# A different hand-written step list for the two later passes of a fused Fourier-layer kernel

## Chip, core and metric

The kernel runs on one core of one Trainium2 chip. The metric is the device time of one execution in microseconds; the kernel before was timed three times. One more execution of it was recorded by the hardware profiler, and all rows below come from that one.

## What is computed

64 images of 256 x 256 pixels go through a tokenizer (four Fourier layers with 32 channels), are joined with 77 text tokens of width 256, and pass through one attention layer and one feed-forward layer that only the better-scored half of the tokens enter. Cut to what matters here:

```python
for i in range(4):                                   # v: [64, 32, 256, 256]
    x_ft = rfft2(v)
    out_ft[:, :, :12, :12]  = einsum('bixy,ioxy->boxy', x_ft[:, :, :12, :12], W1)
    out_ft[:, :, -12:, :12] = einsum('bixy,ioxy->boxy', x_ft[:, :, -12:, :12], W2)
    x1 = irfft2(out_ft)
    x2 = einsum('bcxy,cd->bdxy', v, w_w[i]) + w_b[i]
    v  = x1 + x2
    v  = (v - mean(v)) * rsqrt(var(v) + 1e-5) * bn_g[i] + bn_b[i]    # over all 64 images
    if i < 3: v = relu(v)
h = einsum('bcxy,cu->bxyu', v, q_w) + q_b            # then text, attention, feed-forward
```

Everything is float32.

## The kernel before

An image with its 32 channels is 8.4 MB, so the 64 images stay in DRAM (`vd`, two copies used in turn) and stream through the core once for each of three passes, `layer(0)`, `layer(1)` and `layer(2)`. Between passes, `mix` (line 409) multiplies the kept frequencies with the layer's weights and derives the normalisation. Pass 0 makes its input from the raw pixels and only stores. Passes 1 and 2, the later passes, load every image and store every image. After them comes the tail (line 930 on): attention and feed-forward, which loads the last result once.

**One image in a later pass.** It is cut into eight tiles t = 0 to 7 of [128 partitions, 2048 numbers], 1 MB each. `run` (line 784) gives each step a short name:

- `ld` t (line 631) loads a tile into a buffer of pool `li` (four buffers, name `vin`) as two DMAs of 512 KB on SyncE's queue (SP).
- `sp` h, `spT` h (lines 637, 646) expand the mixed frequencies (`ams`) along x and transpose them on VectorE into `y_`; half h serves four tiles.
- `pre` t (line 655) adds the inverse transform along y (L661, 16 matmul instructions) and the channel product of the loaded tile (L672, 32 instructions) in PSUM.
- `evA` t, `evB` t (line 679) rectify one half each from PSUM into `vo`, a buffer of pool `lo`. The suffix says where: `.a` is ScalarE (L684), `.d` is VectorE (L686). These are the rectified chunks.
- `st` t (line 690) stores the tile to DRAM as two DMAs of 512 KB, also on SP (L693).
- `turn` t (line 695) transposes it on VectorE into half of `t32`, a buffer of pool `lt` that holds two tiles. These are the transposed pairs.
- `prod` t, `sqA`, `sqB` (lines 703, 715) multiply the tile with the next layer's weights (L709) and sum the squares on ScalarE (L720).
- `y` k, k = 0 to 7 (line 724), sum the forward transform along y over all eight tiles (L731), and `half`, `zt0`, `zt1`, `x`, `xo`, `xs` (lines 738 to 782) finish and store the kept frequencies. `am` (line 622) loads and scales the mixed frequencies of a later image.

**Order.** No scheduler orders a pass: `tc.manual_schedule()` (line 838) keeps the program's order on every engine. That order is the text `ORDER[1]` (line 135), which is walked once per image index b (line 802). A mark `@1` runs a step for image b+1, `@-1` for image b-1. Each of TensorE (PE), VectorE (DVE), ScalarE (ACT) and SP has its own queue and takes its own steps in the list's order; an instruction whose data or buffer is not ready holds up all that follow on its engine.

**What makes a step wait.** PSUM is a ring of four two-bank slots (`take`, line 580); `pre`, `prod` and `y` take two, `sp` and `x` one, and the steps that read a slot empty give it back. A load waits until the `pre` that used the same `vin` buffer four loads earlier has read it. An eviction waits until the earlier tile in its `vo` buffer has been stored (landed in DRAM), turned and multiplied. A store waits for its two evictions. In addition, SP's DMAs use eight completion semaphores in turn, and each DMA waits for the one eight places earlier, so that at most eight are under way. In the compiled order of the kernel before this stands as a wait on `DMAHW0` to `DMAHW7` at each DMA.

The pools that matter are opened at line 540: `("lo", 4)` for `vo` and `("lt", 6)` for `t32`, in all three passes.

Of the kernel before, what the change touches and what calls it, by code (L numbers as in the profile page):

```python
# [34 lines left out]
def _tables():  # L35
# [97 lines left out]
    "evB7.a evA7.a prod5 sqB5 prod6 sqA6 st4 x@-1 sqB6 turn6 sqA5 pre1@1 st7 xo@-1 pre0@1 "  # L133
    "evA1.a@1 evB1.d@1 evB0.a@1 xs@-2 evA0.d@1 prod7 sqB7 turn7 sqA7 prod1@1 sp1@1 sqA1@1 "
), (
    "pre5 sqB7@-1 zt1@-1 sqA7@-1 pre6 evA5.a ld2@1 st4 evB5.d st5 turn4 evA6.a prod5 x@-1 "
    "evB6.a sqB5 prod6 sqA5 xo@-1 turn5 pre2@1 sqA6 turn6 sqB6 prod4 evA2.a@1 evB2.d@1 "
    "sqB4 ld0@1 ld7 sqA4 pre0@1 evB0.d@1 ld3@1 prod2@1 st6 evA0.a@1 turn2@1 sqB2@1 sqA2@1 "
    "pre3@1 ld1@1 evA3.a@1 st2@1 evB3.d@1 pre7 evB7.d prod3@1 ld5@1 evA7.a sqA3@1 turn7 "
    "pre1@1 st0@1 am@2 sqB3@1 prod0@1 evA1.a@1 evB1.d@1 sqA0@1 st7 sp1@1 st1@1 ld4@1 y0 "  # L140
    "spT1@1 y1 ld6@1 turn0@1 turn3@1 xs@-2 y2 sqB0@1 prod1@1 y3 sqB1@1 sp0@2 y4 sqA1@1 "
    "spT0@2 y5 y6 st3@1 turn1@1 y7 half.a pre4@1 zt0 prod7 evB4.d@1 evA4.a@1 "
)]

_TABLES, _GRIDS = _tables()
# [7 lines left out]
def tile_fno_fusion_transformer(ctx: ExitStack, tc: tile.TileContext, a, cst_d, grid_d, out):  # L153
    nc = tc.nc
    x = a["x"].rearrange("b x y o -> b x (y o)")
# [369 lines left out]
    def layer(i, st, src, dst, acc):  # L525
# [7 lines left out]
        with ExitStack() as cx:  # L533
            def pool(name, bufs, **kw):
                return cx.enter_context(tc.tile_pool(name=name, bufs=bufs, **kw))
# [1 line left out]
            ip = pool("li", 2 if i == 0 else 4, reuse_waits="tile")  # L537
            op, yp, cp, xp, zp, tp = (
                pool(n, k, reuse_waits="tile")
                for n, k in (("lo", 4), ("ly", 1), ("lc", 1), ("lx", 2), ("lz", 1), ("lt", 6))  # L540
            )
            pp = pool("lp", 1, space=PSUM)
            rv = cp.tile([128, 4, C], F32, name="rv")
# [135 lines left out]
            def ev(h):  # L679
                def run(b, t, e):  # L680
                    key = "pre", b, t
                    to = vo[b, t].rearrange("p (n r) y -> p n (r y)", r=2)[:, 2 * h:2 * h + 2]
                    if e == "a":
                        nc.scalar.activation(to, ring[key][h][1], AF.Relu)  # L684
                    else:
                        nc.vector.tensor_scalar(to, ring[key][h][1], 0.0, None, ALU.max)  # L686
                    close(key, h)
                return run
# [92 lines left out]
            def xs(b, n, e):  # L781
# [3 lines left out]
                am=am, lx=lx, ld=ld, sp=sp, spT=spT, pre=pre, evA=ev(0), evB=ev(1), st=st_, turn=turn,  # L785
# [23 lines left out]
    for i in range(L):  # L809
# [26 lines left out]
        if i < L - 1:  # L836
            acc = const.tile([128, 16 * B], F32, name="acc") if acc is None else acc
            with tc.manual_schedule():
                layer(i, st, vd[(i + 1) % 2], vd[i % 2], acc)
# [374 lines left out]
```

## Time and profile before

| quantity | value |
|---|---|
| median of 3 timed runs | 11689.47 us (11686.08 to 11699.61) |
| the profiled execution | 11646.77 us, span of its instructions 11645.0 us |
| pass 1: first and last `half` (one per image) | at 2995.2 and 5806.4 us |
| pass 2: first and last `half` | at 6032.6 and 8845.3 us |
| busy share of the span: PE, DVE, ACT, POOL | 92%, 73%, 56%, 13% |
| 3200 to 5600 us (53 images of pass 1): PE, DVE, ACT busy | 2299, 1804, 1445 us of 2400 |
| the same: DMA share, GB/s | 0.98, 379 |
| 6100 to 8500 us (pass 2): DMA share, GB/s | 0.98, 379 |

The page gives the whole execution: busy time of each engine, the span in 40 slices, the costliest groups of instructions. A group's row has the line, engine, operation, tiles, count, then busy time and mean duration, then the idle time of the engine just before and what ended it. The windows view gives the same quantities for chosen stretches; its last two columns are the share of time in which the 16 DMA engines were moving packets, and what they moved. The timeline has one row per run of equal instructions: start, duration, engine, line, operation.

### The profile page before, as it was taken

The page shows a single profiled execution, that of the slowest core. Times are in us where ns is not written, and L with a number is a line of the kernel's source. Part 1 is how long each engine was busy: PE and PEld are TensorE (multiplying, and loading weights), DVE is VectorE, ACT ScalarE, POOL GpSimd, SP SyncE. Part 2 cuts the span into 40 slices and gives each one's busy share as a digit, 9 for nine tenths or more (in the row PEclk, how much of TensorE's full clock was granted, in tenths as well). Part 3 has the DMA queues.
Part 4 walks back from the last instruction along what each step waited for, and adds up shares of the span by engine and source line. Part 5 has one row for each costly group of instructions (what it writes and reads, how often), then busy time and mean ns, then how long its engine had stood idle before and what let it go on. Part 6 is the DMA issues. An engine that isn't in the chain of part 4 may idle for free. (4 is left out here: it accounts for less than half of the span.)

```text
span 11645.0 us, 408456 instructions
## 1 busy us (share of the span) xinstructions
PE 10694.7 (92%) x182038; PEld 5785.2 (50%) x182038; DVE 8456.8 (73%) x10405; ACT 6495.3 (56%) x10697; POOL 1461.2 (13%) x2243
## 2 busy tenths in 40 slices
PE   6999999997999999999969999999996999999998
PEld 3444444444444444444434444444443566666666
DVE  5877787877777777777767777777775666666665
ACT  5666676666556656565655656556564333333333
POOL 0100000011000000000010000000001233333333
PEclk7999999998999999999979999999997999999999
DMA  7656565657999999999989999999998655555553
GB/s 230 224 217 222 220 225 217 224 218 234 362 378 383 383 377 376 381 377 381 371 300 381 382 383 376 376 376 383 379 375 285 260 218 221 232 230 218 225 232 141
DMA packets 964095, 3485.49 MB, mean 299 GB/s; under 512 B 142104, under 2 KB 191640, under 8 KB 891032
## 3 DMA queue, kind: packets, MB, share of 16 engines
q1 hardware_dynamic: 906112, 3376.23, 75.4%
q0 software_dynamic: 49072, 79.40, 3.0%
q8 instruction: 1424, 23.33, 0.8%
q10 hardware_dynamic: 7144, 3.72, 0.1%
q14 instruction: 343, 2.81, 0.1%
HBM read 1761.87 MB, written 1696.92 MB: 297 GB/s over the span
## 5 line engine op out<-in xcount | busy, mean ns | idle before, releaser
L720 ACT ACTIVATE ring<-ring 128x1024 f32<-128x1024 f32 x3072 | 3116.3, 1015 | 1211.3 <-PE ring L709 1143.6
L698 DVE STREAM_TRANSPOSE t<-vo 128x2048 f32<-128x2048 f32 x1536 | 3464.2, 2285 | 20.5 <-DVE vo L686 0.5
L709 PE MATMUL ring<-vo,w 32*32 32x512 f32 x49152 | 2463.4, 611 | 233.3 <-ACT vo L684 218.8
L686 DVE TENSOR_SCALAR vo<-ring 128x1024 f32<-128x1024 f32 x1280 | 1544.7, 1221 | 1455.4 <-PE ring L672 800.0
L684 ACT ACTIVATE vo<-ring 128x1024 f32<-128x1024 f32 x1792 | 1791.2, 1022 | 1238.7 <-DMA v<-vo 489.1
L731 PE MATMUL ring<-t,cst 32*32 32x512 f32 x49152 | 2070.8, 599 | 44.0 <-issue 37.9
L709 PEld LDWEIGHTS ring<-vo,w 32*32 32x32 f32 x49152 | 804.4, 103 | 1242.1 <-ACT vo L684 518.1
L609 POOL TENSOR_TENSOR ams<-ams,bns 48x512 f32<-48x512 f32 x384 | 401.0, 1044 | 7781.0 <-DMA ams<-mix 7293.6
L731 PEld LDWEIGHTS ring<-t,cst 32*32 32x32 f32 x49152 | 913.3, 103 | 918.4 <-issue 611.5
L661 PE MATMUL ring<-cst,y 24*128 24x256 f32 x16384 | 1226.3, 402 | 74.9 <-DVE vo L686 59.5
L672 PE MATMUL ring<-vin,ws 32*32 32x512 f32 x32768 | 1276.4, 602 | 17.8 <-issue 11.8
L661 PEld LDWEIGHTS ring<-cst,y 24*128 24x128 f32 x16384 | 786.5, 184 | 988.5 <-DVE vo L686 389.4
L649 DVE STREAM_TRANSPOSE y<-ring 128x1024 f32<-128x1024 f32 x384 | 761.2, 1982 | 327.2 <-PE ring L641 326.2
L661 PE MATMUL ring<-mv,y 29*128 29x256 f32 x8192 | 717.2, 411 | 37.0 <-ACT ring L720 19.6
L765 PEld LDWEIGHTS ring<-cst,zt 128*128 128x128 f32 x4608 | 580.5, 207 | 206.8 <-ACT vo L684 113.9
L661 PEld LDWEIGHTS ring<-mv,y 29*128 29x128 f32 x8192 | 462.8, 189 | 372.9 <-ACT ring L720 210.8
L765 PE MATMUL ring<-cst,zt 128*128 128x96 f32 x4608 | 613.0, 294 | 7.3 <-DVE zt L749 7.3
L741 ACT COPY half<-ring 128x1024 f32<-128x1024 f32 x192 | 194.3, 1012 | 725.8 <-PE ring L731 725.8
L1163 POOL DMA_DIRECT2D out_dram<-o x1024 | 511.0, 507 | 658.6 <-DVE o L1158 617.5
L720 ACT ACTIVATION_READ_ACCUMULATOR ring<-ring 128x1 f32 x3072 | 585.3, 191 | 0.0
L749 DVE STREAM_TRANSPOSE zt<-ring 128x1024 f32<-128x1024 f32 x192 | 377.7, 1967 | 244.5 <-PE ring L731 244.5
L641 PE MATMUL ring<-ams,cst 49*128 49x512 f32 (+1 forms) x1536 | 451.1, 642 | 112.6 <-POOL ams L609 38.5
(367 smaller groups left out, 9784.5 us busy)
## 6 DMA issues: line engine op xcount, KB each, us to landing
v<-vo SPq DMA_DIRECT2D x3072, 512.0 KB, 8.0
vin<-v SPq DMA_DIRECT2D x2048, 512.0 KB, 9.1
ch<-v SPq DMA_DIRECT2D x512, 1024.0 KB, 12.4
mix<-ob SPq DMA_DIRECT2D x96, 512.0 KB, 5.7
ams<-mix SPq DMA_DIRECT2D x384, 96.0 KB, 7.9
xin<-in_x_dram SPq DMA_DIRECT2D x16, 1024.0 KB, 6.0
mv<-in_x_dram POOLq DMA_DIRECT2D x256, 64.0 KB, 9.2
out_dram<-o POOLq DMA_DIRECT2D x1024, 16.0 KB, 3.0
```

What stands on the lines that cost most here:

```text
L641: nc.tensor.matmul(ps[:, n, :], lhsT=EX[hv, 128 * h:128 * h + 128], rhs=ams[b % 2][hv], start=True, stop=True, skip_group_check=True,)
L649: nc.vector.transpose(y_[b, h].rearrange("p q c -> p c q"), ring[key][0][1].rearrange("p n (c k) -> p (n c) k", k=32),)
L661: nc.tensor.matmul(ps[n][:, 256 * r:256 * r + 256], lhsT=y_[b, t // 4][32 * n:32 * n + K, q:q + 4, :].rearrange("p q c -> p (q c)"), rhs=m ...
L672: nc.tensor.matmul(ps[n][32 * j:32 * j + 32], lhsT=ws[32 * n:32 * n + 32], rhs=v[32 * n:32 * n + 32, 2 * j:2 * j + 2, :], start=False, sto ...
L684: nc.scalar.activation(to, ring[key][h][1], AF.Relu)
L686: nc.vector.tensor_scalar(to, ring[key][h][1], 0.0, None, ALU.max)
L698: nc.vector.transpose(t32[b, t // 2][:, :, 8 * (t % 2):8 * (t % 2) + 8, :].rearrange("p y s c -> p s y c"), vo[b, t].rearrange("p s (y l) ...
L709: nc.tensor.matmul(ps[n][32 * j:32 * j + 32], lhsT=w4[i + 1][32 * n:32 * n + 32], rhs=vo[b, t][32 * n:32 * n + 32, 2 * j:2 * j + 2, :], st ...
L720: nc.scalar.activation(ps, ps, AF.Square, accum_out=acc[:, at:at + 1])
L731: nc.tensor.matmul(ps[n][32 * j:32 * j + 32], lhsT=FYT[32 * n:32 * n + 32, k, :], rhs=t32[b, j][32 * n:32 * n + 32, k].rearrange("p s c -> ...
L765: nc.tensor.matmul(ps[:, 0, 96 * g:96 * g + 96], lhsT=zt_[:, h, k0:k0 + 4, :].rearrange("p k c -> p (k c)"), rhs=FX[:, h, 48 * r:48 * r + ...
L1163: nc.gpsimd.dma_start(out[b, 64 * n + 16 * g:64 * n + 16 * g + 16].rearrange("(p t) d -> p t d", t=2), o[32 * g + 8 * n:32 * g + 8 * n + 8 ...
```

## The change

`ORDER[1]`, the list for passes 1 and 2, is replaced, and in those passes `lo` gets five buffers instead of four and `lt` five instead of six. Pass 0, `mix` and the tail keep their code. The new list holds the same steps, so that all matmuls, transposes, squares and DMAs stay the same in number and size. Of an image's sixteen evictions eight are marked `.d` and eight `.a`; before, seven and nine.

```diff
 ), (
-    "pre5 sqB7@-1 zt1@-1 sqA7@-1 pre6 evA5.a ld2@1 st4 evB5.d st5 turn4 evA6.a prod5 x@-1 "
-    "evB6.a sqB5 prod6 sqA5 xo@-1 turn5 pre2@1 sqA6 turn6 sqB6 prod4 evA2.a@1 evB2.d@1 "
-    "sqB4 ld0@1 ld7 sqA4 pre0@1 evB0.d@1 ld3@1 prod2@1 st6 evA0.a@1 turn2@1 sqB2@1 sqA2@1 "
-    "pre3@1 ld1@1 evA3.a@1 st2@1 evB3.d@1 pre7 evB7.d prod3@1 ld5@1 evA7.a sqA3@1 turn7 "
-    "pre1@1 st0@1 am@2 sqB3@1 prod0@1 evA1.a@1 evB1.d@1 sqA0@1 st7 sp1@1 st1@1 ld4@1 y0 "
-    "spT1@1 y1 ld6@1 turn0@1 turn3@1 xs@-2 y2 sqB0@1 prod1@1 y3 sqB1@1 sp0@2 y4 sqA1@1 "
-    "spT0@2 y5 y6 st3@1 turn1@1 y7 half.a pre4@1 zt0 prod7 evB4.d@1 evA4.a@1 "
+    "ld6 ld2@1 evB1.a evA1.d prod7@-1 sqA7@-1 turn0 st0 pre4 sqB7@-1 prod0 evB4.d evA4.a "
+    "sqB0 sp0@1 ld7 pre5 spT0@1 sqA0 prod3 evA5.d turn1 evB5.a zt1@-1 pre6 sqA3 sqB3 "
+    "evB6.a pre2@1 evA6.a st1 prod5 evB2.a@1 turn6 turn4 x@-1 sqA5 sqB5 evA2.a@1 xo@-1 "
+    "prod1 ld3@1 st4 ld0@1 pre7 st5 sqA1 sqB1 evA7.a prod4 turn5 evB7.d pre3@1 sqA4 turn7 "
+    "sqB4 y0 evA3.d@1 y1 xs@-1 ld1@1 st7 st6 ld4@1 evB3.d@1 y2 y3 prod6 am@2 y4 ld5@1 "
+    "st2@1 turn2@1 y5 sqA6 sqB6 st3@1 y6 turn3@1 y7 zt0 pre0@1 half.a evA0.d@1 prod2@1 "
+    "evB0.d@1 sp1@1 sqA2@1 sqB2@1 spT1@1 pre1@1 "
 )]
...
-                for n, k in (("lo", 4), ("ly", 1), ("lc", 1), ("lx", 2), ("lz", 1), ("lt", 6))
+                for n, k in (("lo", 5 if i else 4), ("ly", 1), ("lc", 1), ("lx", 2), ("lz", 1), ("lt", 5 if i else 6))
```

## The prediction, as put on record before the changed kernel was run

> **What bounds the kernel now.** I read the page first, for the stages.
>
> ```profile
> span 11645.0 us, 408456 instructions
> ...
> DMA  7656565657999999999989999999998655555553
> GB/s 230 224 217 222 220 225 217 224 218 234 362 378 383 383 377 376 381 377 381 371 300 381 382 383 376 376 376 383 379 375 285 260 218 221 232 230 218 225 232 141
> ```
>
> Slices of 291 us: from the eleventh to the thirtieth (passes 1 and 2, with `mix` between) DMA stands at 9 tenths or more and moves some 380 GB/s; elsewhere 220. The change touches only these passes. Their length per image: `half` runs once per image, and its 53 executions from 3224.2 to 5580.7 us give 2356.5/52 = **45.3 us**; pass 2 gives the same (6124.3 to 8478.2). Two passes of 64 images make 128 x 45.3 = 5800 us, half the span.
>
> Then the windows view, on one image cut by eye where the DMA rate changes (columns: stretch, length, PE, PEld, DVE, ACT, POOL busy, clock, DMA share, GB/s).
>
> ```profile
> 4010.00:4037.00 27.00, 24.38 (x534) 10.03 (x520) 19.62 (x12) 12.19 (x21) 2.09 (x2) 1.00 1.03 413
> 4037.00:4044.50 7.50, 7.24 (x185) 3.32 (x192) 6.68 (x5) 4.59 (x8) 0.00 (x0) 1.00 0.58 226
> 4044.50:4056.00 11.50, 11.50 (x248) 6.34 (x221) 7.31 (x5) 9.96 (x17) 0.00 (x0) 1.00 1.00 356
> 4056.00:4083.50 27.50, 26.42 (x609) 12.12 (x584) 22.45 (x13) 14.06 (x22) 2.09 (x2) 1.00 1.03 412
> ```
>
> DMA is full at 413 GB/s, then starves for 7.5 us (226 GB/s), then moves only 356 at full share while it recovers. So the passes are DMA-bound with one hole per image. SP's timeline shows who makes the hole.
>
> ```profile
> 4029.65 1.51 SPq L635 DMA_DIRECT2D vin<-v  x2
> 4039.58 4.50 SPq L693 DMA_DIRECT2D v<-vo  x4
> 4044.18 4.34 SPq L635 DMA_DIRECT2D vin<-v  x6
> ```
>
> In the old list the order is st3, ld2, **st4, st5**, ld0, ld7, ld3. After ld2 SP issues nothing for 8.4 us: it waits for the store of tile 4, whose `pre4` stands after y7; ScalarE evicts it at 4038.5. Then six loads come in a row. The wait view of SP for 3200 to 5600 us (53 images) puts this at the top (total us, times, longest):
>
> ```profile
> SPq L693 <- ACT vo L684: 426.1, 109, 7.4
> SPq L693 <- DMA v<-vo: 283.3, 315, 2.1
> ```
>
> The second row is only the limit of eight DMAs under way, normal in a full queue. The first, 8.0 us per image, is SP waiting for evictions. And why are they late? From the groups of the same stretch (idle time, then what ended it):
>
> ```profile
> L684 ACT ACTIVATE vo<-ring 128x1024 f32<-128x1024 f32 x476 | 477.9, 1023 | 312.2 <-PE ring L672 183.2 <-DMA v<-vo 117.3 <-DMA vin<-v 2.7
> L686 DVE TENSOR_SCALAR vo<-ring 128x1024 f32<-128x1024 f32 x370 | 448.9, 1223 | 442.6 <-PE ring L672 323.7 <-DMA v<-vo 114.3 <-DMA vin<-v 2.0
> ```
>
> Both evictors sit idle 117.3/53 = **2.2 us per image** until an earlier store has landed, because `vo` has four buffers. It is a loop: store late, buffer late, eviction late, `pre` late, next store late.
>
> **What the Trainium skill says.** "DMA: Bandwidth & Descriptors", section Anatomy of one DMA: DMA engines do not wait on semaphores; a wait is on the issuing sequencer before dispatch. The trace agrees: the engines drain and stand empty while SP holds st4. Its section Where 436 GB/s comes from puts a core's HBM limit near 358 GB/s and a lone core's measurement at 425; this trace shows 413 in a full stretch, and I use that. "Perfetto Trace Analysis", section Identifying the Most-Contended Engine: matmul busy time is no measure of nearness to the limit. It agrees: PE is 96% busy here (2299 of 2400 us), yet waits, so I cost PE by distances between starts.
>
> **The change, part by part.** *DMA floor.* The bytes stay. At 413 GB/s instead of the mean of 379, an image takes 45.3 x 379/413 = **41.6 us**; no order can beat that, so at most 3.7 us per image can be won, 474 us in all.
>
> *The fifth `vo` buffer.* I count, in SP's order, how many load or store steps stand between the store that frees a buffer and the store of the next tile in it; each is 1.05 MB, 2.54 us at 413 GB/s. Old, four buffers: st3 to st5 has 2 between (5.1 us, from which landing, an eviction of 1.22 us and issue go off), st2 to st1 3, st6 to st7 4. New, five: the smallest is st1 to st7 with 5 (12.7 us), then st2 to st4 with 7. So the 2.2 us of waiting for landed stores should go. What was hidden under it: little, since PE stood behind it (323.7 us of DVE's idle is the next link). Gain taken: 2.2, bounds 0 (the evictors wait for PE instead) and 2.2 plus the rest of the hole.
>
> *SP's new order.* ld6 ld2' st0 ld7 st1 ld3' st4 ld0' st5 xs ld1' st7 st6 ld4' am ld5' st2' st3' (' is the next image). Loads come at most two steps in a row (old: three), stores follow evictions that ended long before: st0, st1 and st6 stand a quarter of an image or more behind theirs. The tightest is st7, right after `pre7`. A load's buffer is still the fourth back; with the PE walk below laid against 2.6 us per SP step, each is free about 3.6 us or more before the queue needs it, and st7's data about 3 us. The slow recovery at 356 GB/s cost 11.5 x (1 - 356/413) = 1.6 us in the image shown. The trace doesn't say whether it comes from the hole or from the six loads; with either gone it should shrink. Bounds 0 to 1.6; I book none of it beyond the 2.2.
>
> *PE's order.* Distances between starts, unhindered, in the PE timeline: `pre` 1.08 + 0.88, `prod` behind a `pre` 1.49 (otherwise 1.07), x 2.85, `sp` 1.06, a `y` step about 1.03. An image: 8 x 1.96 + 6 x 1.49 + 2 x 1.0 + 2.85 + 2 x 1.06 + 8 x 1.03 = **39.9 us** in both lists. Walking the new list with ScalarE's 1.02 us per half, VectorE's 1.22 and 2.28 per `turn`, I add the waits of PE for a slot: behind evA1 0.3, sq7 0.2, evB4 0.3, ev5 0.3, ev6 0.3, sq1 0.5, ev7 0.2, turn7 0.4, zt0 0.5, evA0 0.4, others under 0.2: 3 at most, less what the bank-by-bank start hides, 2.2 taken. PE's own loop so needs about **42.2 us**, less than 45.3 and close to the DMA floor.
>
> *One eviction moved from ScalarE to VectorE.* +1.22 us on VectorE (1804/53 = 34.0, to 35.3 of 45.3), -1.02 on ScalarE (27.3 to 26.3). VectorE still has about 8 us spare, in pieces; I take +0.2 us per image for a piece that isn't covered, bounds 0 and 1.2.
>
> *Five pairs instead of six.* The old list turned tiles of the next image before y7; the new one only turn2' and turn3', and the pair they take was last read by the previous image's y7, about 40 us earlier. Nothing, bounds 0 and 0. *Start and end of a pass:* both lists spread an image over neighbouring indices; 0, bounds -20 and +20 us in all.
>
> *Sum.* 45.3 - 2.2 + 0.2 = **43.3 us** per image, 2.0 x 128 = 256 us less. The profiled execution of 11646.8 becomes 11391. The median of the timed runs stands 42.7 us above that execution; I carry this over: 11689.5 - 256 = **11433**.
>
> **Rivals.** *The hole closes wholly.* PE's loop of 42.2 us sets the pace just above the DMA floor: 3.1 x 128 = 397 us less, **11293**. For it: no step in the new SP order comes right after its data but st7. Against: it leaves no room for either loop to wait for the other.
>
> *The hole only moves.* The buffer wait becomes a wait for PE, or the 356 GB/s stays; 0.7 us per image is won, **11600**. For it: PE is the largest releaser of both evictors already (183 and 324 us), and 2.2 us of waits in PE's loop is my count, not a row.
>
> *Slower.* One place: turn6, turn4 and turn5 stand in a row on VectorE ahead of evB7, 3 x 2.28 = 6.8 us. They are covered by prod5, x, prod1 and pre7 (1.49 + 2.85 + 1.07 + 1.96 = 7.4 us), and turn6 needs both halves of tile 6 from ScalarE, behind a row of five ScalarE steps. The margin is about 0.9 us. What it is late beyond that goes to evB7, then pre3, turn7, y0 and st7. It decides against the change from about 2.9 us late (0.9 margin + the 2.0 won); at 3.9 us an image takes 46.3, **11817**. Against it: ScalarE idles 2400 - 1445 of 2400 us, so rows of five seldom run that late.
>
> **Chances.** Forecast (11390 to 11500) 0.55; hole closes 0.20; hole moves 0.15; slower 0.10. A difference under 0.2% (23 us) can't be told from none here. Faster takes the first two and 0.12 of the third: 0.87; same 0.03; slower 0.10. Range: the forecast, the third case up to 11640, and down to 11310, where the PE count's lower end and the DMA floor leave 0.08 out; the slower case is left out too.
>
> **What would show it.** Right: `half` comes every 43.3 us; the evictors' idle by "DMA v<-vo" falls from 117 us per 2400 to under 20; SP's wait for ScalarE evictions falls below half; DMA moves 390 to 400 GB/s over the passes. The full closure shows 405 or more. A moved hole shows the same DMA rate, with a long SP wait at st7 or a load. The slower case shows a hole before y0 and VectorE busy in turns while L686 is due. My sum is wrong if landed stores still hold up evictions, or if recovery slowness stays without a hole.

## The result, and the profile after

The changed kernel takes **12512.31 us** (median of 4 runs, 12479.99 to 12539.62). The kernel before, run beside it, took 11687.77 us. The ratio is 1.071, 95% interval 1.067 to 1.075. The forecast was 11433. From one `half` to the next an image of a later pass takes 51.8 us, where it took 45.3 and 43.3 was forecast; 128 x 6.5 us = 832 us is the whole loss of 825. (In the kernel before, the last `half` of pass 1 starts at 5838.5 and of pass 2 at 8878.9 us; the table above has the last but one.)

The page of the changed kernel, its slices (312 us each) as before:

```profile
span 12489.4 us, 407557 instructions
...
PEclk8999999998999999999979999999999799999999
DMA  7556555658999998999989989899989755555553
GB/s 233 220 217 224 212 213 218 223 219 293 333 335 338 335 331 326 328 331 332 333 275 338 338 330 332 327 328 333 330 327 329 256 219 226 232 229 220 220 229 151
```

In the later passes DMA moves some 332 GB/s instead of 380; outside them little changed. The windows of one image (same columns as before) show how:

```profile
4504.00:4528.00 24.00, 23.27 (x457) 9.87 (x457) 19.73 (x12) 15.61 (x24) 0.00 (x0) 0.93 0.76 257
4528.00:4540.00 12.00, 7.76 (x140) 4.78 (x142) 6.60 (x5) 6.73 (x12) 0.00 (x0) 0.94 0.97 389
4540.00:4556.00 16.00, 14.75 (x334) 8.41 (x334) 9.04 (x5) 3.83 (x8) 2.09 (x2) 0.83 0.98 349
```

The thin stretch is longer than the 7.5 us hole of before, and in the second window it is TensorE that stands idle (7.76 of 12 us busy). SP's timeline of that image:

```profile
4527.32 1.70 SPq L693 DMA_DIRECT2D v<-vo  x2
4531.23 0.32 SPq L782 DMA_DIRECT2D xh<-xo  x1
4531.64 0.91 SPq L635 DMA_DIRECT2D vin<-v  x2
4539.66 2.84 SPq L693 DMA_DIRECT2D v<-vo  x4
...
4547.80 3.92 SPq L693 DMA_DIRECT2D v<-vo  x4
4558.96 6.29 SPq L635 DMA_DIRECT2D vin<-v  x4
```

The first row is st5. SP issues xs and ld1', then nothing for 7 us until st7 (4539.66), and again nothing for 7 us ahead of ld6 and ld2' (4558.96). What SP waits for, 3400 to 5800 us (46 images), and the two evictors' groups of the same stretch:

```profile
SPq L635 <- PE ring L672: 729.7, 236, 10.2
SPq L693 <- ACT vo L684: 286.3, 58, 7.3
```

```profile
L686 DVE TENSOR_SCALAR vo<-ring 128x1024 f32<-128x1024 f32 x371 | 445.8, 1222 | 424.3 <-DMA v<-vo 247.6 <-PE ring L672 176.7
L684 ACT ACTIVATE vo<-ring 128x1024 f32<-128x1024 f32 x370 | 373.4, 1022 | 395.9 <-PE ring L672 203.4 <-DMA v<-vo 192.0
```

SP's wait for evictions fell from 8.0 to 6.2 us per image (286.3/46), but a wait of loads for `pre` (729.7/46 = 15.9, where it was 96.1/53 = 1.8) now leads. The evictors' wait for landed stores was to vanish; it grew from 2.2 to 5.4 us per image on VectorE and 4.2 on ScalarE. The wait view says what sort of wait it is:

```profile
DVE vo L686 <- DMA v<-vo: 247.6, 47, 6.9
...
ACT vo L684 <- DMA v<-vo: 192.0, 47, 5.8
```

47 times in 46 images: not many small waits, but one long one per image. The timelines of VectorE, ScalarE and TensorE show which:

```profile
4526.64 6.70 DVE L698 STREAM_TRANSPOSE t<-vo 128x2048 f32<-128x2048 f32 x3 [0.21 <-ACT vo L684]
...
4538.61 1.02 ACT L684 ACTIVATE vo<-ring 128x1024 f32<-128x1024 f32 x1 [4.36 <-DMA v<-vo]
4538.63 1.22 DVE L686 TENSOR_SCALAR vo<-ring 128x1024 f32<-128x1024 f32 x1 [5.29 <-DMA v<-vo]
...
4539.69 2.30 PE L661 MATMUL ring<-cst,y 24*128 24x256 f32 x16 [4.24 <-ACT vo L684]
...
4541.92 2.01 PE L672 MATMUL ring<-vin,ws 32*32 32x512 f32 x32
```

The turns of tiles 6, 4 and 5 end at 4533.3. Then evA7 and evB7 stand still until a store lands at 4538.5, and TensorE's next `pre` with them. That store is st5, issued 4527.32 to 4529.02, of the same image. It is so throughout: in all of 56 successive images of pass 1, evA7 and evB7 start 0.1 to 0.6 us after the second half of st5 has landed.

**Why st5.** The compiled program tells which tile's buffer each tile gets, by address and by the waits of its evictions. It isn't a strict turn, in either kernel (x <- y: tile x gets the buffer that tile y had; ' is the next image):

```
before, four buffers:  7<-4  5<-3  6<-1  1'<-2'  4'<-0'  3'<-6  0'<-5  2'<-7 of the image before
after, five buffers:   7<-5  6<-0  4<-2  5'<-7   1'<-6   0'<-4  3'<-1  2'<-3
```

The pool gives tile 7 the buffer of tile 5, whose store stands one xs and one load ahead of st7 on SP and is issued some 10 us (median) before it lands. Tiles 5 and 7 share one buffer, and the other six have four. Over the whole run the page's median from issue to landing of a store is 8.4 us; the three list steps between st5 and evA7 can't hide such a wait.

### The profile page after: what moved, and what is told of

Its sections match the earlier page's. It is cut to its first block, busy times and chain, and to the rows that moved or that the text cites. A ratio compares the mean times of both kernels' runs of the same rounds, so it can differ in the third digit from the quotient of the medians.

```text
span 12489.4 us, 407557 instructions
## 1 busy us (share of the span) xinstructions
PE 10953.7 (88%) x182038; PEld 6027.5 (48%) x182038; DVE 8629.1 (69%) x10533; ACT 6356.3 (51%) x10569; POOL 1461.0 (12%) x2243
## 5 line engine op out<-in xcount | busy, mean ns | idle before, releaser
L698 DVE STREAM_TRANSPOSE t<-vo 128x2048 f32<-128x2048 f32 x1536 | 3474.2, 2291 | 64.7 <-ACT vo L684 43.7
L686 DVE TENSOR_SCALAR vo<-ring 128x1024 f32<-128x1024 f32 x1408 | 1687.5, 1220 | 1548.4 <-DMA v<-vo 673.5
L684 ACT ACTIVATE vo<-ring 128x1024 f32<-128x1024 f32 x1664 | 1667.6, 1022 | 1578.7 <-DMA v<-vo 728.4
L731 PE MATMUL ring<-t,cst 32*32 32x512 f32 x49152 | 2135.4, 625 | 181.5 <-issue 177.8
L661 PE MATMUL ring<-cst,y 24*128 24x256 f32 x16384 | 1350.9, 430 | 547.8 <-ACT vo L684 493.1
L661 PEld LDWEIGHTS ring<-cst,y 24*128 24x128 f32 x16384 | 873.8, 198 | 1456.9 <-ACT vo L684 731.7
L731 PEld LDWEIGHTS ring<-t,cst 32*32 32x32 f32 x49152 | 1066.0, 106 | 1057.7 <-issue 730.6
L672 PE MATMUL ring<-vin,ws 32*32 32x512 f32 x32768 | 1347.5, 662 | 17.1 <-issue 16.8
L962 PE MATMUL hp<-ch,win 128*32 128x512 f32 x4096 | 472.5, 601 | 7.6 <-DMA ch<-v 7.5
```

What stands on the lines that cost most here:

```text
L661: nc.tensor.matmul(ps[n][:, 256 * r:256 * r + 256], lhsT=y_[b, t // 4][32 * n:32 * n + K, q:q + 4, :].rearrange("p q c -> p (q c)"), rhs=m ...
L672: nc.tensor.matmul(ps[n][32 * j:32 * j + 32], lhsT=ws[32 * n:32 * n + 32], rhs=v[32 * n:32 * n + 32, 2 * j:2 * j + 2, :], start=False, sto ...
L698: nc.vector.transpose(t32[b, t // 2][:, :, 8 * (t % 2):8 * (t % 2) + 8, :].rearrange("p y s c -> p s y c"), vo[b, t].rearrange("p s (y l) ...
L731: nc.tensor.matmul(ps[n][32 * j:32 * j + 32], lhsT=FYT[32 * n:32 * n + 32, k, :], rhs=t32[b, j][32 * n:32 * n + 32, k].rearrange("p s c -> ...
L962: nc.tensor.matmul(hp[32 * g:32 * g + 32], lhsT=win[:, 7 - t:39 - t], rhs=ch[:, g], start=False, stop=t == 7, skip_group_check=True,)
```

## The experiments

All ratios are to the kernel before, run beside each, with 95% intervals.

**e1_rot5: the changed kernel, its five buffers in strict turn.** Its pool has one set of five fixed tiles.

```diff
+            nvo, vob = [0], [op.tile([128, 8, S], F32, name=f"vo{n}") for n in range(5)] if i else []
...
-                vo[b, t] = op.tile([128, 8, S], F32, name="vo")
+                if i:
+                    vo[b, t] = vob[nvo[0] % len(vob)]
+                    nvo[0] += 1
```

> The new list, with the five rectified-chunk buffers handed out by hand in strict turn (tile 7 then takes tile 1's buffer instead of tile 5's). Theory (the buffer hand-out): evA7/evB7 no longer wait for st5, PE has no idle of 4 us and its clock stays full; half every 43.5 to 45.5 us, 11400 to 11750 us, evictors' idle by landed stores under 20 us per 2400. Rival (the list itself, its long y stretch and PE loop, is what costs): little changes, half every 50 us or more, over 12250 us.

Measured 11858.94 us, 1.014 (1.012 to 1.016); 46.7 us per image. From the waits of 3400 to 5800 us:

```profile
DVE vo L691 <- DMA v<-vo: 11.1, 9, 2.6
```

The landed-store waits are all but gone, as the prediction had it for a strict turn, and 653 of the 825 us with them. But the time stays above the 11400 to 11750 of the theory, and the list is still slower than the old one.

**e2_newlist_oldpools and e3_oldlist_newpools: list and pools apart.** e2 has the new list with `("lo", 4)` and `("lt", 6)`; e3 has the old list with 5 and 5.

> The new list with the old pools (four chunk buffers, six pairs). Theory (buffer hand-out): with four, tile 2 takes tile 5's buffer, whose store stands later in the list than tile 2's eviction; worse than the changed kernel, 12800 to 13500 us. Rival (the list alone costs, buffers don't matter): within 1% of 12512.

> The old list with the new pools (five chunk buffers, five pairs). Theory: buffers as such do no harm; tile 7 then takes tile 6's buffer; 11550 to 11750 us. Rival (five pairs instead of six cost): VectorE's turns wait for y7 and the time rises by 1% or more, over 11800.

e2: 13556.4 us, 1.159 (1.156 to 1.162). e3: 12645.95, 1.082 (1.080 to 1.084). Each half alone is worse than both together. e2 is just above its theory's range; e3's theory, that the new pools do no harm, fell. In e2 tile 2' takes the buffer of tile 5, and x waits behind its eviction; in e3 the old list's turns of the next image, which run ahead of y7, wait for a pair, while ScalarE's wait for landed stores is down to 4.4 us. The waits of 3400 to 5800 us, first e2, then e3:

```profile
ACT vo L684 <- DMA v<-vo: 520.3, 76, 12.4
...
PE ring L765 <- ACT vo L684: 388.4, 40, 12.2
```

```profile
DVE t L698 <- PE ring L731: 467.9, 45, 13.2
```

With the new list no turn waits for y7: there five pairs cost nothing, as predicted.

**e5_warm: TensorE kept busy.** TensorE's granted clock was 0.94 in this stage, and the `pre` after the wait took 2.30 + 2.01 us instead of 1.15 + 1.16. The Trainium skill, "TensorE: Matmul & The Clock Gate", Part 1, has the clock halve after an idle activity window and return after a busy one, each of some 3.4 us; the trace agrees, with 54 records of 0.5 from 3400 to 5800 us that last 3.4 or 6.8 us. Here `prod4` is issued five times over to keep TensorE busy:

```diff
-                for k in range(4):
+                for k in [k for _ in range(5 if i and t == 4 else 1) for k in range(4)]:
```

> The changed kernel, with the matmuls of prod4 in the later passes issued five times over (same result, 3.5 us more of PE work just where PE otherwise sits idle behind evA7). If the half clock after that idle stretch is a cost of its own, the clock record shows 0.97 or more in the passes and the time falls by 1.5 to 3.4 us per image, to 12080 to 12320 us. If only the wait costs, it stays within 60 us of 12512 or rises.

Measured 12514.12 us, 1.070 (1.067 to 1.073): no difference. Windows and waits of the stage:

```profile
3400.00:5800.00 2400.00, 2246.65 (x48956) 1127.90 (x48956) 1645.08 (x930) 1223.43 (x1955) 95.96 (x92) 0.98 0.92 332
```

```profile
DVE vo L686 <- DMA v<-vo: 244.2, 46, 7.1
```

TensorE is 94% busy at a clock of 0.98 (20 such records are left), and the store wait is as long as before. The `pre` after the wait takes 2.0 us less (medians), but starts 0.7 us later behind evA7, where the added matmuls overrun; the image is none the shorter, 51.8 us. So the half clock is a consequence of the wait, which costs no measurable time here. What takes up the remaining 1.3 us was not followed. TensorE's busy share isn't what sets the pace of the changed kernel.

**e16_st5_only and e13_st5_early: the store earlier.** Pools as changed; e16 exchanges st4 and st5, e13 also turn5 and turn6. The pool's choice stays 7<-5.

```diff
-    "prod1 ld3@1 st4 ld0@1 pre7 st5 sqA1 sqB1 evA7.a prod4 turn5 evB7.d pre3@1 sqA4 turn7 "
+    "prod1 ld3@1 st5 ld0@1 pre7 st4 sqA1 sqB1 evA7.a prod4 turn5 evB7.d pre3@1 sqA4 turn7 "
```

> The changed kernel with its pools, and two exchanges in the list: st5 with st4, and turn5 with turn6. The pool hands out the same buffers as before this edit (tile 7 takes the buffer of tile 5 of the same image), but st5 now stands three steps (ld0', pre7, and the former place) and turn5 some eight steps earlier ahead of evA7. Theory: the loss comes from evA7 and evB7 waiting for the store and the turn of tile 5, about 5 us once per image; st5 is issued ahead of ld0' and lands about 2.5 us earlier or more, so the wait falls to 1 to 2.5 us and the time to 12000 to 12250. Rival: the loss comes from something else in the new list (the y run, the loads behind it) and the store wait only stands on top; then it stays within 1% of 12512.

> The changed kernel with its pools and one exchange, st5 with st4; turn5 stays behind evA7. Tile 7 still takes the buffer of tile 5. If the landing of st5 alone is what evA7 and evB7 wait for, the time is that of e13_st5_early (11882) within 0.5%; if turn5 stands right behind it as the next wait, it stays above 12100.

e13: 11882.33 us, 1.015 (1.012 to 1.018). e16: **11832.65**, 1.014 (1.010 to 1.017). Two words exchanged win back 680 us. e13 wins 630, where 260 to 510 were expected; e16 is as its expectation had it. From e16's waits, 3400 to 5800 us:

```profile
DVE vo L686 <- DMA v<-vo: 34.3, 23, 4.0
...
ACT vo L684 <- DMA v<-vo: 2.9, 6, 1.0
```

The turn of tile 5 is no second wait: e16, which leaves it where it was, is not slower than e13.

**e14_pool_by_hand and e15_by_hand_fair: the pool's order by hand.** Fixed tiles as in e1, but in the pool's order:

```diff
+                    k = [0, 1, 2, 3]
+                    for _ in range(b):
+                        k = [k[2], k[0], k[3], k[1]]
+                    k += [k[2], 4, k[0], 4]
+                    vo[b, t] = vob[k[t]]
```

> As e1_rot5, but the five fixed vo buffers are handed out by hand in the order that the pool chose for the changed kernel (tiles 5 and 7 of every image in one buffer, the other six in turn in four). In one thing it still differs from the pool: each half tile waits only for the store of its own half. Theory A: the order is the cause; then the time is again 12512 within 1%, less what the half-wise wait saves (at most one 512 KB store, 1.3 us per image or 160 us). Theory B: what e1_rot5 won came from the half-wise waits or from fixed tiles instead of a pool; then it stays near 11859.

> As e14_pool_by_hand, with turn5 written ahead of evA7 in the list, which leaves every engine's own order as it is. In e14_pool_by_hand turn5 stood behind evA7 and, with fixed buffers, read the first half of tile 7 in place of tile 5, and waited for it: a changed computation and another wait than the pool's. Here evA7 waits for turn5 and st5 as in the changed kernel. Theory: the order of handing out is the cause of the loss; then 12300 to 12550 (12512 less at most 160 us for half-wise waits). Rival: fixed buffers or half-wise waits are what e1_rot5 won by; then below 12000.

e14: 12835.5 us, 1.097 (1.095 to 1.100). It is no fair copy, for the reason that e15's expectation gives. e15: **12505.81**, 1.070 (1.067 to 1.074), the changed kernel's time again, with fixed tiles. So the order of handing out is the cause of the 5.1 us per image that e1 wins back, and neither the pool as such nor the width of its waits.

**e4_oldlist_rot4: the old list, its four buffers in strict turn.** The edit is e1's, on the kernel before.

> The old list with its four vo and six pair buffers, but the four vo buffers handed out in strict turn. Theory A: the order of handing out matters as much as the number: in strict turn tile 3' takes the buffer of tile 5 and tile 7 that of tile 6, whose stores and turns stand closer than with the pool's own choice (7 from 4, 5 from 3, 6 from 1), so the wait for landed stores grows beyond 2.2 us per image and the time goes to 11800 to 12000. Rival: strict turn is the better rule for any list; then it is below 11690.

Measured **11657.45** us (20 runs), 0.9974 (0.9965 to 0.9983), against 11696.49: the fastest version that does all the work, and the only one of them below the kernel before. The theory expected it slower and fell; the time is the rival's, that strict turn is the better rule, as it was for the new list in e1. Its groups, 3400 to 5600 us, and SP's first wait, 3200 to 5600:

```profile
L689 ACT ACTIVATE vo<-ring 128x1024 f32<-128x1024 f32 x440 | 445.2, 1023 | 266.0 <-PE ring L673 255.3 <-DMA vin<-v 3.8 <-DMA v<-vo 1.8
L691 DVE TENSOR_SCALAR vo<-ring 128x1024 f32<-128x1024 f32 x342 | 418.8, 1225 | 405.0 <-PE ring L673 356.8 <-DMA v<-vo 26.6 <-DMA vin<-v 13.7
```

```profile
SPq L698 <- ACT vo L689: 424.9, 125, 7.9
```

This tests the forecast's main term by itself. In the kernel before, both evictors waited 2.2 us per image for landed stores; here it is 26.6 and 1.8 us in some 49 images, 0.5 and under 0.1. The image went from 45.33 to 45.17 us: **0.2, not 2.2**. Most of the idle time only changed its name to "PE ring" (ScalarE 183.2/53 = 3.5 to 255.3/49 = 5.2 us per image, VectorE 6.1 to 7.3), and SP's wait for evictions, the hole, is as long as it was (426.1 before). So the hole isn't the doing of the buffer wait.

**e11_old_less and e7_rot5_half, e12_rot5_less: which resource sets the pace.** Work is left out, of TensorE (y1, y3, y5) or of DMA (the second store of each tile).

```diff
+                if i == 1 and k in (1, 3, 5):
+                    return
...
-                for n in range(2):
+                for n in range(1 if i == 2 else 2):
```

> The kernel before with less work, of another kind in each later pass: pass 1 leaves out y1, y3 and y5 (three of the eight terms of the forward transform along y, 96 matmuls or about 3.7 us of TensorE per image), pass 2 leaves out the second 512 KB store of each tile (a quarter of its DMA traffic). The output is not the reference's. Theory A (the prediction's): the passes are bound by DMA and a hole in it; then pass 1 stays near 45.3 us per image, since its SP order and store waits are the same, and pass 2 falls to 43 us or below. Theory B: TensorE's own loop of some 45 us sets the pace and the hole in the DMA stream is only its spare time; then pass 1 falls to about 42 us, near the DMA floor of 41.6, and pass 2 stays within 0.5 us of 45.3.

> As e1_rot5, but pass 2 stores only the first 512 KB of each tile's 1 MB (half of that pass's stores are left out, so that the last result is incomplete and the tail reads old data). It compares pass 1 with pass 2 in one execution. Theory A: TensorE's gaps in the y run come from instruction blocks that wait behind data in full DMA engines; then they are 1.4 us per image in pass 1 and near 0 in pass 2, and pass 2 runs at the pace of TensorE's own loop, which the prediction put at 42.2 us per image (39.9 without waits). Theory B: the supply is slow by itself; then the gaps stay in pass 2 and an image takes 44 us or more there. Whole time about 11300.

> The new list with five vo buffers in strict turn (e1_rot5), with y1, y3 and y5 left out in both later passes, and in pass 2 also the second 512 KB store of each tile. The output is not the reference's. Pass 2 of e7_rot5_half, with the halved stores alone, took 45.8 us per image against 46.8. Theory B (TensorE's loop sets the pace): pass 1 falls to about 43 us (3.7 us of steps and about 1 us of supply gaps less, held up by DMA from 42 us on), and pass 2 to 41 us or below. Theory A (the order of loads and stores makes DMA slow by itself): pass 1 stays above 45.5 us at 368 GB/s or less.

These are single runs; the time per image is from start to start of y0 over 55 images:

| us per image | all work | stores halved | y1, y3, y5 out | both |
|---|---|---|---|---|
| old list | 45.3 | 44.4 (e11, pass 2) | 44.1 (e11, pass 1) | - |
| new list, strict turn | 46.8 | 45.8 (e7, pass 2) | 43.8 (e12, pass 1) | 41.7 (e12, pass 2) |

The two passes of e11:

```profile
3400.00:5200.00 1800.00, 1685.06 (x33933) 743.47 (x33947) 1383.06 (x775) 1111.64 (x1756) 85.62 (x82) 0.98 1.00 390
6400.00:8400.00 2000.00, 1932.90 (x41761) 940.60 (x41761) 1536.95 (x856) 1233.08 (x1936) 94.05 (x90) 1.00 0.81 292
```

Neither theory of e11 holds as written. In the old list neither resource bounds alone: some 3.6 us of TensorE's work less (three steps of 1.2) brings 1.2, a quarter less traffic 0.9. The new list leans on TensorE: the same y steps bring 3.0 there, the traffic 1.0, and e12 comes within 0.8 us of its theory B. e7's theory B holds for the image, but its whole time of 11798 us was expected near 11300. At only 283 GB/s e7 still needs 45.8 us, where the prediction had 42.2 for TensorE's loop.

**e9_x_in_y and e8_pre0_early: the rest of the loss.** TensorE idles inside the y run of e1, 3400 to 5800 us (51 images), with nothing to wait for:

```profile
4541.44 4.01 PE L736 MATMUL ring<-t,cst 32*32 32x512 f32 x106
4547.71 1.94 PE L736 MATMUL ring<-t,cst 32*32 32x512 f32 x11 [2.26 <-issue]
```

```profile
PE ring L736 <- issue: 80.7, 58, 2.6
```

In the kernel before, 3400 to 5600 us (some 49 images), it is 0.3 us per image against 1.6:

```profile
PE ring L731 <- issue: 13.9, 20, 1.4
```

In the trace, DMA queue 8 ("instruction") brings blocks of 16 KB, of about 1 us each. There are 48 gaps over 0.4 us between matmuls of the y steps from 3400 to 5600 us, and every one ends 1.2 to 1.7 us after such a block has landed; in the kernel before all 16 do (1.25 to 1.55). Of moments picked at random only some 9 in 100 lie so. Between two blocks TensorE starts some 256 matmuls and weight loads (median). The Trainium skill, "Runtime: NRT & Kernel Launch", section Instruction fetch mechanics, gives the same 256 instructions per block, and calls the fetch mostly hidden. In the y run of the new list it isn't by these times: a y step has 64 instructions in 1.0 to 1.2 us, and the new list has eight of them with one `prod` between. e9 puts x, 24 matmuls in 2.85 us, into the run; e8 puts `pre0` of the next image there, because ld6 waits for it. Both are edits of e1. First e9's edit, then e8's:

```diff
-    "evB6.a pre2@1 evA6.a st1 prod5 evB2.a@1 turn6 turn4 x@-1 sqA5 sqB5 evA2.a@1 xo@-1 "
+    "evB6.a pre2@1 evA6.a st1 prod5 evB2.a@1 turn6 turn4 sqA5 sqB5 evA2.a@1 "
...
-    "sqB4 y0 evA3.d@1 y1 xs@-1 ld1@1 st7 st6 ld4@1 evB3.d@1 y2 y3 prod6 am@2 y4 ld5@1 "
-    "st2@1 turn2@1 y5 sqA6 sqB6 st3@1 y6 turn3@1 y7 zt0 pre0@1 half.a evA0.d@1 prod2@1 "
+    "sqB4 y0 evA3.d@1 y1 ld1@1 st7 st6 ld4@1 evB3.d@1 y2 x@-1 y3 xo@-1 prod6 am@2 y4 ld5@1 "
+    "xs@-1 st2@1 turn2@1 y5 sqA6 sqB6 st3@1 y6 turn3@1 y7 zt0 pre0@1 half.a evA0.d@1 prod2@1 "
```

```diff
-    "st2@1 turn2@1 y5 sqA6 sqB6 st3@1 y6 turn3@1 y7 zt0 pre0@1 half.a evA0.d@1 prod2@1 "
-    "evB0.d@1 sp1@1 sqA2@1 sqB2@1 spT1@1 pre1@1 "
+    "st2@1 turn2@1 y5 sqA6 sqB6 pre0@1 st3@1 y6 evA0.d@1 turn3@1 evB0.d@1 y7 zt0 half.a "
+    "prod2@1 sp1@1 sqA2@1 sqB2@1 spT1@1 pre1@1 "
```

> As e1_rot5, with x of the previous image (24 matmuls of 2.85 us in all) moved from behind turn4 into the y run, behind y2, and xo and xs behind it. Theory A: TensorE's instructions arrive in blocks of 16 KB over the same DMA engines, and a run of eight y steps uses them up faster than they arrive; a step with few instructions in the middle gives the next block time to land. Then TensorE's idle time with nothing to wait for inside the y steps (1.4 us per image in e1_rot5, gaps over 0.4 us) falls below 0.5, and the time falls to about 11740 if nothing stands in for it. Theory B: the gaps have another cause, tied to the y steps themselves; then they stay at 1.4 us. Rival: x gone from its old place uncovers turn6, turn4, turn5 ahead of evB7 on VectorE, so that y0 begins late; then the gaps go, but the time stays at 11860 or rises.

> New list, five vo buffers handed out in strict turn (as in e1_rot5, 11859 us), and pre0 of the next image with its two evictions moved from behind zt0 to between y5 and y6. Theory A: what is left of the loss in e1_rot5 is the hole at ld6 and ld2' (2.6 and 1.7 us per image instead of 1.27 per 512 KB), because the buffers of these loads are read by pre0' and pre1' behind the y run; then the hole shrinks, an image takes about 45 us instead of 46.7 and the time is about 11650. Theory B: a full stream of alternating loads and stores without such a cause simply moves 368 GB/s; then 11859 stays within 0.3%. Rival C: the evictions of tile 0 hold up turn3', zt0 and prod2', and the hole moves to st2' or st3'; then 11900 or more.

e9: 11863.47 us, 1.014 (1.011 to 1.017). Its wait, same stretch:

```profile
PE ring L736 <- issue: 18.6, 20, 1.7
```

The gaps fall from 1.6 to 0.4 us per image, so a run of dense steps is what opens them. The time doesn't fall: between starts, `pre` and `prod` take 1.2 us per image more in e9 than in e1. The rival has it right, that x is missed at its old place. e8: 12129.1, 1.038 (1.035 to 1.041), worse. From its groups, 3400 to 5800 us:

```profile
L714 PE MATMUL ring<-vo,w 32*32 32x512 f32 x12640 | 673.1, 611 | 71.8 <-DVE vo L691 61.3 <-issue 10.5
```

`prod2'` now waits for VectorE, busy with the evictions of tile 0: rival C's mechanism. So no experiment here turned the supply gaps into time, and that they are the 1.4 us by which e1 exceeds the kernel before is not shown.

## Why the prediction was wrong

The mechanism was wrong, not only the number. *The fifth vo buffer* is the step that failed, in its count. "I count, in SP's order, how many load or store steps stand between the store that frees a buffer and the store of the next tile in it ... New, five: the smallest is st1 to st7 with 5" takes it that buffers are handed out in strict turn. The pool gives tile 7 that of tile 5, with one load between, so that tile 7's evictions wait 4.2 and 5.4 us per image for st5 to land, where the count had them wait for nothing. This costs 5.1 us per image, 653 (e1) to 680 us (e16) of the 825. The gap between the forecast and the result is 1079 us; this is the largest part of it.

*The same step's gain of 2.2* failed as well: e1 has the waits gone and isn't faster, and on the old list their removal was worth 0.2 us (e4). The working named the right doubt ("PE stood behind it", bound 0) and then took the upper value. "It is a loop: store late, buffer late, eviction late" was argued and is refuted: the hole stayed without the buffer wait.

*PE's order.* For e1 the sum was too small in both terms. (Its own terms add to 39.8, and the waits that it lists by name to 3.4, not "3 at most"; neither slip matters here.) The table sums the distances between starts over 55 images, with gaps over 0.15 us taken out:

| us per image | pre | prod | y | x | sp | sum | gaps | loop |
|---|---|---|---|---|---|---|---|---|
| prediction | 15.7 | 10.9 | 8.2 | 2.9 | 2.1 | 39.9 | 2.2 | 42.2 |
| e1_rot5 | 16.9 | 11.9 | 9.7 | 2.9 | 2.3 | 43.7 | 3.0 | 46.7 |
| kernel before | 17.1 | 11.6 | 9.7 | 2.9 | 2.2 | 43.5 | 1.9 | 45.3 |

The prediction's distances are below the mean ones (`pre` 1.96 against 2.1 us), and idle time of kind "issue", 2.7 of the 3.0 us in e1, was left out. The last row could have been had before the run: TensorE stood visibly idle for only 1.9 us per image, less than the 2.0 that the forecast took off. Steps and gaps always add up to the period, though, so the row doesn't show that TensorE alone needs 43.5: a distance also holds waits under 0.15 us. In pass 1 of e11 the y steps are 3.4 us shorter, but the other steps grow by 1.3 and the gaps by 0.9.

*SP's new order.* "Loads come at most two steps in a row" is right, "the tightest is st7" is right, but its 3 us of slack hung on evB7. The loads' 3.6 us or more of slack is refuted even in e1, where SP waits for `pre` most:

```profile
SPq L636 <- PE ring L673: 595.0, 247, 7.1
```

*DMA floor.* No run with all traffic came near its 41.6 us (45.2 at best, e4), so it was not tested. "So the passes are DMA-bound with one hole per image" is too strong: with a quarter less traffic the old list still needs 44.4 (e11). *Eviction moved, five pairs:* neither shows as a wait with the new list. *What would show it:* all four signs failed. SP's wait for evictions fell, but only from 8.0 to 6.2 us per image. The sign that the prediction named for a wrong sum, "landed stores still hold up evictions", is what the trace shows.

*The rivals.* None had this mechanism. "Slower" looked at the right place, evB7 behind turn6, turn4 and turn5, and gave it the wrong cause: the three turns ran in one go (6.70 us, idle 0.21 ahead), and the buffer was late, not VectorE. Its margin of 0.9 us doesn't come out of the two sums beside it, 7.4 - 6.8 = 0.6.

**Open:** what makes e1 1.4 us per image slower than the kernel before (in the table nearly all of it is gaps, but closing most of those in the y run won nothing in e9), where the time that e9 frees goes in detail, and why e14's other wait costs 2.6% more.

## What to carry to other kernels

Before counting how far apart a buffer's users stand, read from the compiled program which tile gets which buffer; one more buffer in a pool with a hand-written order can bring two neighbours together. Compare that distance with the measured time from issue to landing of a store (8.4 us in the median here, 10 for st5), and try an exchange of two stores before rewriting a list. And before booking an evictor's wait as a gain, look at how long TensorE stands idle per image: where that is as little as the gain (1.9 us here), the wait may only change its name, as in e4.

## What the runs showed of the hardware that was not expected

- By the times of the blocks, TensorE outran its own instruction supply: gaps of up to 2.6 us in the y run, those over 0.4 us each closed 1.2 to 1.7 us after a 16 KB block landed, and fewer when the run was broken up (e9). A quarter less DMA traffic left them nearly as they were (1.6 us per image in pass 1 of e7, 1.4 in pass 2), so that full DMA engines alone don't explain them.
- A high DMA share isn't a full DMA. With a quarter of the traffic gone, e7 shows a share of 0.83 at 283 GB/s, with packets of 4096 bytes of 190 ns in the mean against 173 in its pass 1. In e1 the share is 0.99 at 368 GB/s; in the stretches that end with the landing of a half of ld2' it is still 0.94, at 312 GB/s. Pass 2 of e7:

```profile
6600.00:8600.00 2000.00, 1876.72 (x40427) 952.04 (x40413) 1545.39 (x873) 1148.38 (x1837) 89.72 (x86) 0.99 0.83 283
```

- TensorE's half clock after an idle stretch cost no measurable time where the pace was set by another wait (e5: 12514 us against 12512).
